# Two graph layers on one core: the loads that bring activations back in natural layout move from SyncE's queue to GpSimd's

## The chip, the cores and the metric

The kernel runs on one core of a Trainium2 chip. The metric is the device time of one execution in microseconds (us). The kernel before took 1773.51 us (median of three runs, 1772.94 to 1775.36).

## The reference

The input `x` is 16 batches of 1024 nodes by 128 features, `adj` a 1024 x 1024 matrix, all float32. Two layers, each with a layernorm, a relu and a residual:

```python
h = jnp.maximum(_layernorm(x), 0.0)
x = x + adj @ (h @ weight) + bias                     # layer 0, per batch
h = jnp.maximum(_layernorm(x), 0.0)                   # layer 1: five steps of a gated unit
for _ in range(5):
    m = adj @ h                                       # m_in and m_out are the same product
    av = concatenate([m, m])
    u3 = h @ u3_w.T + u3_b
    z = sigmoid(av @ w3_w.T + w3_b + u3)
    r = sigmoid(av @ w4_w.T + w4_b + u3)
    hv = tanh(av @ w5_w.T + w5_b + (r * h) @ u5_w.T + u5_b)
    h = (1 - z) * h + z * hv
x = x + h
```

Nearly all arithmetic is the product with `adj`, once a step and batch ("aggregation"), and the products with the small weights ("gates").

## The kernel before, in words

**Tiling.** Four batches make a quad; there are four quads. Two quads are in work at a time (`state[0]` and `state[1]`), and their steps alternate: while one quad aggregates, what the other quad's last step left is stored and fetched. One `step` is an aggregation, then the gates of batch pair A, then those of pair B.

**The aggregation** (`aggregate`, matmuls at L504) is a two-level scheme of seven products by seven: 49 small products, numbered by `place(1)` to `place(49)`. Each has two 128 x 128 x 256 matmuls, which the profile shows as four. `adj`'s sums for 40 of the 49 products do not stay in SBUF: they stream from DRAM through `ring`, 12 slots, which are six pairs. One DMA of 512 KB brings a pair (`stream`, 20 pairs an aggregation, 440 in all). It is issued after the second product of a pair, into that pair's slots, so it is needed six pairs later. The last four of an aggregation and the first of the next are put at places in the gates (`GATE_LOADS`).

**Two layouts.** Gates work on `hT` (features on partitions). The aggregation wants the natural layout (nodes on partitions) in `nat[:, k]`, k = 0 to 3 a batch. So after a step VectorE transposes 32 x 32 squares of `hT` (`squares_to_dram`, L669), one DMA of 512 KB stores them to a DRAM scratch (`fn`), and `natural_from` loads the scratch back in four DMAs of 128 KB, each to 32 partitions in runs of 1 KB. Sixteen such loads fill `nat` for one aggregation. Sources are `fn` (a step's result), `ft` and `h` (the layernorm's output of layer 1 and layer 0, parked in DRAM). The output of a finished batch is fetched by the same function into `ho`.

**Who reads nat.** ScalarE copies (L401) and VectorE sums (L238, L241) make the left operands in `big` from it. The first four pieces for the next aggregation are placed in the gates just ahead of it (`GATE_PLACES`: the first copy, of k = 0, at "Az0", the second, of k = 1, at "Az1", the sums of k = 2 and 3 at "Bz1"). The last reads of `nat[:, 0]` and `nat[:, 1]` are the VectorE sums at places 18 and 19 of the running aggregation (`bigs[5]`), those of `nat[:, 2]` and `nat[:, 3]` the ScalarE copies at places 25 and 26 (`bigs[6]`).

**What sets the order.** The author writes out the program order of every engine: `put(k, piece)` hangs a piece on a place and `place(k)` emits it there. `pin` keeps it in that order on its engine. Nothing ties instructions of different engines except semaphores for data and for buffers. All DMAs are issued by SyncE through `dma` (L129), so a DMA that waits holds up those behind it. In a usual step the four groups of loads into `nat` are put at places 48, "Ar0", "Ar1" and "Ar3" of the step that runs (`loads_at`), which is the end of the aggregation and the first gates. GpSimd does only the `pow` of the layernorms (L344), 34 instructions, the last of them at 990 us, and a few set-up instructions.

Of the kernel before, what the change touches and what calls it, by code (L numbers as in the profile page):

```python
# [96 lines left out]
def tile_two_gnn_layers(  # L97
# [9 lines left out]
    nc = tc.nc  # L107
    pin = tc.keep_in_program_order
# [19 lines left out]
    def dma(out, in_):  # L128
        pin(nc.sync.dma_start(out=out, in_=in_))  # L129
# [522 lines left out]
    def by_blocks(hN, k):  # L652
        return hN[bass.ts(k, SQ)].rearrange("y a j e -> y a (j e)")
# [19 lines left out]
    def natural_from(blocks, hN):  # L673

        for k in range(NSQ):
            dma(by_blocks(hN, k), blocks[k])

    parked = {}
    x1s = {}
# [35 lines left out]
    def output(b, blocks):  # L715
        box = {}

        def load():
            box["h"] = flip_tile(f"ho_{b}")
            natural_from(blocks, box["h"])  # L720
            box["x1"] = x_tile(f"1_{b}")
            dma(box["x1"], x1s[b])

        def rest():
            x1 = box["x1"].rearrange("p j (a e) -> p a j e", e=SQ)
            for g in range(NH):
                js = bass.ts(g, CH)
                add(x1[:, :, js], x1[:, :, js], box["h"][:, :, js])

        def store():  # L730
            dma(by_slots(out[b]), box["x1"])

        return load, rest, store
# [244 lines left out]
    def loads_of_next(source, places):  # L978

        for k, at in enumerate(places):  # L980
            put(at, lambda k=k: natural_from(source[k], nat[:, k]))
# [294 lines left out]
```

## Time and profile before

| what | value |
|---|---|
| median of three runs | 1773.51 us |
| the profiled execution's own time | 1770.63 us |
| its span, first to last instruction | 1768.9 us |
| TensorE busy | 1759.2 us, 99% of the span |
| VectorE, ScalarE busy | 1375.1 us (78%), 898.1 us (51%) |
| GpSimd busy | 58.8 us (3%) |
| DMA engines busy, mean of 16 | 70%, 224 GB/s over the span |
| granted TensorE clock | 0.999 |

The span is what the profile sees of one execution; the profiled execution took 1.7 us more than its span. Busy shares are averages over the whole run. A busy DMA share of 1.00 in a window means that all 16 DMA engines had a packet under way all the time.

### The profile page before, as it was taken

The numbers are of one execution on the slowest core, as the hardware profiler recorded it, in microseconds if no ns is written. First come the engines' busy times: TensorE is split into PE (matmuls) and PEld (weight loads), VectorE is DVE, ScalarE is ACT, GpSimd is POOL, SyncE is SP. The second block draws the span as 40 slices with busy tenths as digits, with TensorE's granted clock in tenths as the row PEclk, the third lists the DMA queues.
The fourth block names the chain that finished last, engine by engine and source line by source line (L and its number), as shares of the span: only waits on it lengthen the run. The fifth ranks groups of instructions, "written<-read, shape, count | busy, mean of one in ns | idle before, by whom it ended". The sixth has DMA issues, their size and how long they took to land.

```text
span 1768.9 us, 21409 instructions
## 1 busy us (share of the span) xinstructions
PE 1759.2 (99%) x6438; PEld 1201.1 (68%) x6438; DVE 1375.1 (78%) x2806; ACT 898.1 (51%) x1974; POOL 58.8 (3%) x41
## 2 busy tenths in 40 slices
PE   9999999999999999999999999999999999999998
PEld 3557667588585776858857667585775858667584
DVE  6778888777878687887687968777687777868787
ACT  5246555544555555554455554545455454544544
POOL 3101000000000000000000000000000000000000
PEclk9999999999999999999999999999999999999999
DMA  7499786677496956749749577494866749476684
GB/s 256 157 309 316 228 259 212 181 245 247 127 298 192 284 193 198 237 137 294 226 149 328 177 225 282 151 294 159 248 211 194 252 133 295 166 230 230 193 294 170
DMA packets 169970, 396.88 MB, mean 224 GB/s; under 512 B 18560, under 2 KB 88064, under 8 KB 169856
## 3 DMA queue, kind: packets, MB, share of 16 engines
q1 hardware_dynamic: 169856, 395.52, 70.1%
q8 instruction: 52, 0.85, 0.2%
q14 instruction: 62, 0.51, 0.1%
HBM read 314.44 MB, written 81.00 MB: 224 GB/s over the span
## 4 chain that ended last, share of the span: by engine, by line
PE 96%; DVE 1%; DMA 1%; POOL 1%; ACT 0%; issue 0%; SPq 0%; DVEq 0%; POOLq 0%
PE a L504 27%; PE c L504 14%; PE b L504 7%; PE a_a L504 3%; PE pr_2B L808 2%; PE pr_1B L808 2%; PE pr_0B L808 2%; PE pr_3B L808 2%; PE pr_3A L808 2%; PE pr_2A L808 2%; PE pr_0A L808 2%; PE pr_1A L808 2%; PE pr_4A L808 2%; PE pr_4B L808 2%; PE a_a L620 2%; PE pv_3A L808 2%
## 5 line engine op out<-in xcount | busy, mean ns | idle before, releaser
L504 PE MATMUL a<-ring,big 128*128 128x256 f32 x1120 | 287.9, 380 | 0.3 <-ACT Z L523 0.3
L523 ACT COPY Z<-a 128x256 f32<-128x256 f32 x480 | 177.0, 371 | 193.2 <-PE a L504 193.0
L241 DVE TENSOR_TENSOR Z<-Z,taps 128x512 f32<-128x512 f32 (+1 forms) x264 | 144.6, 554 | 166.3 <-ACT taps L523 166.1
L504 PE MATMUL c<-ring,little 128*128 128x256 f32 x960 | 246.5, 379 | 0.0
L504 PEld LDWEIGHTS a<-ring,big 128*128 128x128 f32 x1120 | 212.2, 190 | 37.4 <-issue 8.1
L241 DVE TENSOR_TENSOR mT<-mT,Z 128x1024 f32<-128x1024 f32 x154 | 188.3, 1223 | 22.9 <-ACT Z L523 17.3
L504 PEld LDWEIGHTS c<-ring,little 128*128 128x128 f32 x960 | 182.2, 190 | 25.1 <-ACT taps L523 0.2
L523 ACT COPY taps<-c 128x256 f32<-128x256 f32 x280 | 103.6, 370 | 116.3 <-PE c L504 111.5
L504 PE MATMUL a<-resident,little 128*128 128x256 f32 x560 | 143.8, 379 | 0.0
L504 PE MATMUL a<-ring,little 128*128 128x256 f32 x560 | 143.7, 379 | 0.0
L504 PE MATMUL b<-ring,big 128*128 128x256 f32 x560 | 143.7, 379 | 0.0
L504 PEld LDWEIGHTS a<-resident,little 128*128 128x128 f32 x560 | 106.3, 190 | 14.7 <-ACT Z L523 0.3
L504 PEld LDWEIGHTS a<-ring,little 128*128 128x128 f32 x560 | 106.4, 190 | 14.4
L504 PEld LDWEIGHTS b<-ring,big 128*128 128x128 f32 x560 | 106.5, 190 | 14.4
L669 DVE STREAM_TRANSPOSE sq<-hT_all 128x512 f32<-128x512 f32 x152 | 98.6, 687 | 0.0
L241 DVE TENSOR_TENSOR little<-big 128x256 f32<-128x256 f32 x154 | 64.2, 417 | 21.4 <-ACT big L401 21.2
L401 ACT COPY big<-nat 128x512 f32<-128x512 f32 x132 | 80.7, 614 | 0.1
L523 ACT COPY taps<-b 128x256 f32<-128x256 f32 x140 | 52.0, 371 | 55.4 <-PE b L504 54.5
L238 DVE TENSOR_TENSOR little<-little,big 128x256 f32<-128x256 f32 x154 | 65.4, 425 | 6.7
L238 DVE TENSOR_TENSOR little<-big 128x256 f32<-128x256 f32 x154 | 64.3, 418 | 0.0
L238 DVE TENSOR_TENSOR little<-big,little 128x256 f32<-128x256 f32 x154 | 64.3, 418 | 0.0
L523 ACT COPY mT<-a 128x256 f32<-128x256 f32 x80 | 29.8, 372 | 48.3 <-PE a L504 48.3
(282 smaller groups left out, 2911.1 us busy)
## 6 DMA issues: line engine op xcount, KB each, us to landing
ring<-rd SPq DMA_DIRECT2D x440, 512.0 KB, 5.8
fn<-sq SPq DMA_DIRECT2D x76, 512.0 KB, 3.9
nat<-fn SPq DMA_DIRECT2D x256, 128.0 KB, 5.7
x1d<-xt SPq DMA_DIRECT2D x16, 512.0 KB, 5.4
sqt<-ft SPq DMA_DIRECT2D x16, 512.0 KB, 6.9
xt<-x1d SPq DMA_DIRECT2D x16, 512.0 KB, 7.0
xt<-in_x_dram SPq DMA_DIRECT2D x15, 512.0 KB, 5.7
out_dram<-xt SPq DMA_DIRECT2D x14, 512.0 KB, 7.6
```

Of the source, the lines that this page charges most:

```text
L238: pin(nc.vector.tensor_sub(o, a, b))
L241: pin(nc.vector.tensor_add(o, a, b))
L401: return [lambda i=i: pin(nc.scalar.copy(made_of(k, i), part(a, b, i))) for i in range(2)]
L504: nc.tensor.matmul(bank, l, right[:, c, :], start=opens and c == 0, stop=c == SB - 1, skip_group_check=True,)
L523: pin(nc.scalar.copy(to, bank))
L620: nc.tensor.matmul(bank, left[:, c, :], right[c // SB][:, c % SB], start=p in (1, 2, 5) and c == 0, stop=c == CH - 1, skip_group_check=True,)
L669: pin(nc.vector.transpose(squares_of_half(sq, g), transposed_half(hT, g)))
L808: nc.tensor.matmul(bank, w_sb[:, w, :], moving, start=start, stop=stop, skip_group_check=True)
```

## The change

One line of `natural_from` (L673 to L676). The four loads of each group are issued from GpSimd's queue:

```diff
     def natural_from(blocks, hN):
 
         for k in range(NSQ):
-            dma(by_blocks(hN, k), blocks[k])
+            pin(nc.gpsimd.dma_start(out=by_blocks(hN, k), in_=blocks[k]))
```

The instructions of TensorE, VectorE and ScalarE and their order stay as they were. SyncE issues 384 DMAs less (256 `nat<-fn`, 48 `nat<-ft`, 32 `nat<-h`, 48 `ho<-fn`), and GpSimd issues them in the same order among themselves, between its `pow` instructions. Twelve loads of the last step (`ho_last`, in `fetch`) stay on SyncE.

## The prediction

> **What bounds the kernel now.** I read the page from the top: busy shares, the chain that ended last, then the waits of TensorE.
>
> ```profile
> span 1768.9 us, 21409 instructions
> PE 1759.2 (99%) x6438; PEld 1201.1 (68%) x6438; DVE 1375.1 (78%) x2806; ACT 898.1 (51%) x1974; POOL 58.8 (3%) x41
> PE 96%; DVE 1%; DMA 1%; POOL 1%; ACT 0%; issue 0%; SPq 0%; DVEq 0%; POOLq 0%
> ```
>
> TensorE (PE) is the chain; it idles 9.7 us in all. The waits of PE between 115 and 1725 us, which is from the first streamed aggregation to the last, are one line:
>
> ```profile
> PE a L504 <- ACT Z L523: 0.3, 1, 0.3
> ```
>
> So there is nothing to win where the changed loads work: a faster load can take away 0.3 us. The question is what it can cost. PE never waits for `ring` or `nat` today, so I look for how near it is to waiting, in one usual step (aggregation from 1146.6 to 1189.0 us, gates to 1223.2). First, all engines by stretches (columns: length, PE, PEld, DVE, ACT, POOL busy, clock, DMA share, GB/s); a quiet aggregation's window and one of nearly pure natural loads follow:
>
> ```profile
> 1146.60:1162.90 16.30, 16.30 (x77) 14.37 (x76) 14.76 (x28) 7.38 (x19) 0.00 (x0) 1.00 0.80 263
> 1162.90:1172.50 9.60, 9.60 (x47) 8.45 (x46) 6.43 (x14) 5.10 (x13) 0.00 (x0) 1.00 1.02 305
> 1172.50:1178.50 6.00, 6.00 (x29) 5.29 (x28) 3.62 (x9) 2.61 (x7) 0.00 (x0) 1.00 0.96 366
> 1199.00:1223.20 24.20, 24.20 (x57) 10.64 (x56) 20.25 (x34) 12.57 (x20) 0.00 (x0) 1.00 0.18 65
> ...
> 840.00:856.40 16.40, 16.40 (x78) 14.47 (x77) 11.15 (x24) 6.70 (x18) 0.00 (x0) 1.00 0.68 215
> 1184.00:1187.50 3.50, 3.50 (x18) 3.08 (x17) 3.21 (x5) 1.59 (x5) 0.00 (x0) 1.00 0.80 183
> ```
>
> The DMA engines are full in the middle of an aggregation and nearly idle (0.18) in the gates. Then SyncE's timeline there, and the landing times of the DMAs on `ring` (min/median/max):
>
> ```profile
> 1178.21 0.43 SPq L129 DMA_DIRECT2D out_dram<-xt  x1
> 1178.69 10.44 SPq L129 DMA_DIRECT2D nat<-fn  x12
> 1189.24 0.38 SPq L129 DMA_DIRECT2D ring<-rd  x1
> 1189.71 1.80 SPq L129 DMA_DIRECT2D nat<-fn  x4
> ```
>
> ```profile
> DMA to landing us min/median/max: 2.4/5.7/10.3
> ```
>
> The natural loads leave SyncE from 1178.7 to 1191.5, behind the aggregation's other DMAs.
>
> **Part 1: what SyncE loses.** 384 issues at 0.42 us (median of `nat<-fn`), 161 us of SyncE's time. It is worth 0 to PE, by the wait list: `ring` DMAs already land before their use. The last four `ring` DMAs of an aggregation no longer stand behind `nat` groups and go out some us earlier; they are needed in the next aggregation, 30 us later. Nothing.
>
> **Part 2: when the loads start.** On SyncE a load's place in the program is also its time. On GpSimd hardly anything stands ahead of it (34 `pow`, all before 992 us), so it starts when its data and its room are ready:
>
> ```profile
> 1162.92 0.69 DVE L238 TENSOR_TENSOR big<-nat,big 128x512 f32<-128x512 f32 x1
> 1163.86 0.68 DVE L238 TENSOR_TENSOR big<-nat,big 128x512 f32<-128x512 f32 x1
> ```
>
> ```profile
> 1169.49 0.62 ACT L401 COPY big<-nat 128x512 f32<-128x512 f32 x1
> 1170.35 0.62 ACT L401 COPY big<-nat 128x512 f32<-128x512 f32 x1
> ```
>
> These are the last reads of `nat[:, 0]`, `[:, 1]` and of `[:, 2]`, `[:, 3]`. The last source, the `fn` store issued at 1155.2, lands 5.9 us later, at 1161.1. So the sixteen loads can start at 1163.6 instead of 1178.7: **15 us earlier, out of the slack stretch and into the full one**. The `ho` loads (issued at 1160.95, at place 16) move the other way: their room comes free in the gates before, where DMA is idle.
>
> **Part 3: what an issue costs on GpSimd.** The trace shows no DMA from GpSimd. From below, SyncE's 0.42 us for the same DMA; from above, GpSimd's own `pow` on 128 x 8, 1.65 us median (up to 2.45 beside VectorE). Neither row is nearer in kind, so I take their geometric middle, sqrt(0.42 x 1.65) = 0.83, call it 0.9 us. Both ends go into the range. Sixteen take 14.4 us, 1163.6 to 1178.
>
> The Trainium skill, *DMA: Bandwidth & Descriptors*, "Specifications", gives about 1 us to the first byte from GpSimd against 0.6 us from SyncE; if that were the price of each issue, the excess of 4.6 us worked out below would be 4.1 (estimate), and the sum hardly different. No row here shows it.
>
> **Part 4: the DMA engines in that stretch.** A `ring` DMA of 524 KB comes every 42.4/20 = 2.12 us and takes a share of 0.68 in the quiet window: 1.44 us of all engines. A natural load takes 0.80/183 GB/s x 131 KB = 0.57 us: 16 are 9.2 us. In 14.4 us the ring asks 0.68 x 14.4 = 9.8, the loads 9.2: 19.0 in 14.4, **4.6 us too much**. Someone's data comes later by that.
>
> What the ring can bear: its DMA goes out when a pair is done and is needed five pairs later, 5 x 2.12 = 10.6 us. It lands after 5.7 in the median: slack 4.9 us. The longest landing of 10.3 us left 0.3.
>
> The 22 aggregations by what else moves:
> - Six (the first, the last, four quiet ones): 4.6 is under 4.9 or there is no such load. 0.
> - Eight with a layernorm's store. Its first tile, four 128 KB DMAs, comes at place 22, 2.3 us of DMA time; four of the eight also store `x1d`, 1.44. Excess 6.9 or 8.3, beyond the slack 2.0 or 3.4: 4 x 2.0 + 4 x 3.4 = 21.6 us.
> - Eight with an output. `ho` has left, the `xt<-x1d` load stays: 4.6 + 1.44 = 6.0, beyond the slack 1.1: 8.8 us.
>
> Together **30.4 us, if the ring bears all of the delay, and 0 if the natural loads bear it**. No row shows two busy queues side by side. I take half, 15.2 us, as neither queue has a claim over the other here. Delay of the natural loads themselves is free: they land by 1183 or so, and the first reader is the copy for "Az0" at 1197.4.
>
> The skill's same page, "Queues, rings and completion order", says each DMA engine goes round between the queues that have work, packet by packet. That would be equal shares, so nearer to the half than to either end; by it the sum stays 15.2. Against the change speaks *SBUF — State Buffer*, "Who interferes with whom": VectorE in a two-port mode keeps GpSimd from writing descriptors. It also says `tensor_tensor`, most of VectorE's work here, has no such mode, so I expect little of it. If it stretched an issue to 2 us, the loads would be spread over 32 us and most of the 15 us would go.
>
> **Sum.** 1770.6 (this execution) + 15.2 - 0.3 = 1785.5. The median of the runs is 2.9 above the profiled execution, so 1788.
>
> **Rivals.**
> 1. *Hidden* (not slower). GpSimd issues slowly enough: at 1.65 us an issue the sixteen take 26 us, in which the ring asks 18.0 and the loads 9.2: 27.2 in 26, an excess of 1.2 us that every slack covers; or the ring's packets go first. It decides from about 1.3 us an issue: there the excess is 2.5, only the four fullest aggregations pass their slack, by 1.3 us, and half of 4 x 1.3 is 2.6 us, too little to tell from no change. For it: 4.9 us median slack. Against: the eight output aggregations are at share 1.02 already. 1773.5, PE's floor. Chance 0.30.
> 2. *The loads don't move*: an unseen wait holds GpSimd, and they leave near their old time. Then nothing changes: 1773.5. The program order on GpSimd shows none. Chance 0.06.
> 3. *GpSimd is the bound.* The last loads are due before the sums on `nat[:, 2:4]` at 1215.4. From 1170.1, less 5.5 us landing, that leaves 39.8 us for eight: it decides from 5 us an issue. At 6 us, sixteen take 96 us in a step of 76.6: 20 steps x 19 = 390 us more, 2160 us. The longest GpSimd row is 2.45 us. Chance 0.02.
> 4. *Faster.* The shorter queue on SyncE, and `ho` gone from the fullest stretch. PE has only 0.3 us to give back there, so over 0.2% needs something I don't see. Chance 0.03.
>
> The forecast, slower by ring stalls, has 0.59. Measurement can tell some 0.2% (3.5 us). Part of the forecast lies under that, so I count it in rival 1: slower 0.61, same 0.36, faster 0.03. The range runs from rival 1 less the spread of the runs (1772) to the full 30.4 us and the spread above (1806).
>
> **What would show it.** In the profile after: `nat` issues on POOL from about place 19, 15 us earlier; their duration (0.9 expected, wrong if over 1.3); DMA share 1.0 from place 19 to the end of the aggregation and lower in the first gates; `ring` landing median above 5.7 with a maximum beyond 10.6; PE waits at L504 for "DMA ring<-rd" of 1 to 4 us in store and output aggregations, none in quiet ones and none for `nat`. If PE's wait list stays at 0.3 us while the loads did move, part 4 is wrong; if the waits name `nat` or `big`, part 3 is.

## The result and the profile after

The changed kernel takes 1854.73 us (median of four runs, 1849.58 to 1855.29), the kernel before, run beside it, 1773.90 us. The ratio is 1.0451, 95% interval 1.0439 to 1.0463: 4.5% slower. The profiled execution of after took 1855.3 us with a span of 1853.4 us, 84.5 us more than the span of before. The forecast was slower, 1788 us, at most 1806.

Page of after: span, busy shares, chain of waits by engine, the two busiest DMA queues.

```profile
span 1853.4 us, 21560 instructions
PE 1788.0 (96%) x6438; PEld 1204.8 (65%) x6438; DVE 1375.8 (74%) x2806; ACT 899.0 (49%) x1974; POOL 269.9 (15%) x425
PE 81%; DMA 15%; DVE 1%; POOL 1%; ACT 1%; issue 0%; SPq 0%; DVEq 0%; POOLq 0%; ACTq 0%
q1 hardware_dynamic: 114560, 345.16, 55.0%
q0 software_dynamic: 18432, 50.36, 10.6%
```

TensorE's work is the same 6438 matmuls, but its share falls from 99% to 96%, and 15% of the chain is now DMA where it was 1%. The 384 moved loads are a queue of their own (q0). TensorE's waits (us in total, times, longest):

```profile
PE a L504 <- DMA ring<-rd: 32.9, 26, 4.6
PE b L504 <- DMA ring<-rd: 8.2, 10, 2.6
PE c L504 <- DMA ring<-rd: 7.2, 3, 4.3
PE a_a L504 <- DMA ring<-rd: 3.2, 4, 1.2
PE a L504 <- ACT taps L523: 2.0, 4, 0.5
```

Where before had one wait of 0.3 us, 45 waits for `ring`, 52.4 us in all (a fifth line of 0.9 us is not shown), stand now. None is for a load into `nat`. The same quiet aggregation in both kernels shows the mechanism. First GpSimd's timeline after (start, us, what, xcount, in brackets its idle time and what ended it), in an aggregation that begins at 418.9 us:

```profile
436.49 4.36 POOL L676 DMA_DIRECT2D nat<-fn  x8 [39.14 <-DVE little L238]
442.74 1.64 POOL L676 DMA_DIRECT2D nat<-fn  x3 [1.89 <-ACT big L401]
444.76 0.55 POOL L676 DMA_DIRECT2D nat<-fn  x1 [0.38 <-DMA nat<-fn]
446.23 1.10 POOL L676 DMA_DIRECT2D nat<-fn  x2 [0.92 <-ACT Z L523]
448.04 0.55 POOL L676 DMA_DIRECT2D nat<-fn  x1 [0.71 <-DMA nat<-fn]
449.09 0.55 POOL L676 DMA_DIRECT2D nat<-fn  x1 [0.50 <-DMA nat<-fn]
```

Then SyncE before, in the same aggregation, which begins at 407.3 us there:

```profile
438.94 6.89 SPq L129 DMA_DIRECT2D nat<-fn  x12
446.12 0.34 SPq L129 DMA_DIRECT2D ring<-rd  x1
446.70 1.96 SPq L129 DMA_DIRECT2D nat<-fn  x4
```

The first load leaves 17.6 us into the aggregation instead of 31.7, 14 us earlier. What DMA makes of it after, the quiet stretch ahead of the loads first (length, PE, PEld, DVE, ACT, POOL busy, clock, DMA share, GB/s):

```profile
418.90:436.50 17.60, 17.60 (x84) 15.51 (x83) 12.42 (x26) 7.21 (x20) 0.01 (x1) 1.00 0.67 210
...
438.00:457.00 19.00, 18.07 (x83) 15.30 (x82) 11.19 (x22) 8.83 (x23) 7.24 (x14) 1.00 1.01 259
457.00:463.30 6.30, 6.04 (x28) 5.01 (x28) 3.55 (x6) 2.23 (x6) 0.00 (x0) 1.00 1.02 393
```

For 19 us all engines are full and move 259 GB/s, `ring` and natural loads together. Then the loads are done, and the same full engines move 393 GB/s: `ring` catching up. Of 259 x 19.0 = 4.92 MB, 2.10 MB are the sixteen loads, so `ring` got 2.82 MB, 5.4 DMAs, where TensorE used up 19.0/2.12 = 9.0 (at the mean of one in 2.12 us). It fell 3.6 DMAs behind, and TensorE stood still in this quiet aggregation too, three times here:

```profile
453.15 1.10 PE L504 MATMUL a<-ring,big 128*128 128x256 f32 x4 [0.41 <-DMA ring<-rd]
...
456.50 1.13 PE L504 MATMUL b<-ring,big 128*128 128x256 f32 x4 [0.52 <-DMA ring<-rd]
...
458.76 1.10 PE L504 MATMUL a<-ring,big 128*128 128x256 f32 x4 [0.26 <-DMA ring<-rd]
```

Landing times (min/median/max) of the `ring` DMAs, then of the 384 moved loads, after:

```profile
DMA to landing us min/median/max: 2.4/6.7/18.6
```
```profile
DMA to landing us min/median/max: 2.7/8.0/11.5
```

A landing of 18.6 us where a `ring` DMA has 10.6 us until it is needed is a stall.

**Where the 84.5 us are.** 52.4 are the waits for `ring`. 15.4 are a half clock: seven stretches, 30.7 us together, in which the granted clock was 0.5 (experiment 7). 3.5 more are waits for ScalarE. 5.0 are longer records of single matmuls outside these stretches, nearly all directly after a wait (worked out from the trace's matmul records). Of the other 8.2, some 7.5 are overlap, from the same records: back to back, a matmul's record begins 0.16 us before the one ahead of it ends, and after each of 46 waits outside the half clock it doesn't. Under 1 us has no name.

### The profile page after: what moved, and what is told of

Its sections match the earlier page's. It is cut to its first block, busy times and chain, and to the rows that moved or that the text cites. A ratio compares the mean times of both kernels' runs of the same rounds, so it can differ in the third digit from the quotient of the medians.

```text
span 1853.4 us, 21560 instructions
## 1 busy us (share of the span) xinstructions
PE 1788.0 (96%) x6438; PEld 1204.8 (65%) x6438; DVE 1375.8 (74%) x2806; ACT 899.0 (49%) x1974; POOL 269.9 (15%) x425
## 3 DMA queue, kind: packets, MB, share of 16 engines
q0 software_dynamic: 18432, 50.36, 10.6%
## 4 chain that ended last, share of the span: by engine, by line
PE 81%; DMA 15%; DVE 1%; POOL 1%; ACT 1%; issue 0%; SPq 0%; DVEq 0%; POOLq 0%; ACTq 0%
PE a L504 21%; DMA ring<-rd 15%; PE c L504 10%; PE b L504 5%; PE pr_3A L808 2%; PE pr_3B L808 2%; PE pr_2B L808 2%; PE pr_1B L808 2%; PE pr_0B L808 2%; PE pr_1A L808 2%; PE pr_0A L808 2%; PE pr_2A L808 2%; PE a_a L504 2%; PE pr_4B L808 2%; PE pr_4A L808 2%; PE a_a L620 1%
## 5 line engine op out<-in xcount | busy, mean ns | idle before, releaser
L504 PE MATMUL a<-ring,big 128*128 128x256 f32 x1120 | 294.9, 386 | 36.7 <-DMA ring<-rd 32.9
L676 POOL DMA_DIRECT2D nat<-fn x256 | 140.4, 553 | 508.0 <-ACT Z L523 268.1
L504 PEld LDWEIGHTS b<-ring,big 128*128 128x128 f32 x560 | 106.4, 191 | 26.9 <-DMA ring<-rd 12.7
L504 PEld LDWEIGHTS a<-resident,little 128*128 128x128 f32 x560 | 107.5, 192 | 15.2 <-ACT Z L523 0.3
L676 POOL DMA_DIRECT2D ho<-fn x48 | 26.2, 552 | 391.6 <-DMA fn<-sq 242.1
L241 DVE TENSOR_TENSOR little<-big 128x256 f32<-128x256 f32 x154 | 64.4, 418 | 21.4 <-ACT big L401 21.4
L344 POOL TENSOR_TENSOR rstd_b<-ve_b,mhalf 128x8 f32<-128x8 f32 x16 | 28.0, 1752 | 279.2 <-DVE ve_b L343 268.2
```

Source lines behind the costliest of these rows:

```text
L241: pin(nc.vector.tensor_add(o, a, b))
L344: pin(nc.gpsimd.tensor_tensor(self.rstd[:, part], self.ve[:, part], mhalf[:, part], ALU.pow))
L504: nc.tensor.matmul(bank, l, right[:, c, :], start=opens and c == 0, stop=c == SB - 1, skip_group_check=True,)
L676: pin(nc.gpsimd.dma_start(out=by_blocks(hN, k), in_=blocks[k]))
```

## The experiments

"Early" below means from place 19 on, as the change does it; "held" means not before the engines reach the place in the program where the group stood. That is not the old time: SyncE ran ahead of the other engines there. In most aggregations the first held load of kernel 1 starts 42.8 to 43.7 us in, where before started it at 31.7 to 35.7. Loss is against the runs of before beside the same kernel. The columns by kind are the lengthening of the aggregations against before, from the first to the last matmul at the aggregation's line, worked out from the trace: four quiet, eight with a layernorm's store, eight with an output. The first and the last aggregation are in no column; the last lost 4.4 us in after, 5.2 in kernel 4 and 7.3 in 5b.

| kernel | median us | loss | ring waits | quiet 4 | store 8 | output 8 |
|---|---|---|---|---|---|---|
| after | 1854.7 | 80.8 | 52.4 | 10.2 | 38.1 | 31.6 |
| 1 all on GpSimd, held | 1784.0 | 10.4 | 0.4 | 2.6 | 1.3 | 0.8 |
| 2 all on SyncE, early | 1870.8 | 97.2 | 67.1 | 6.7 | 39.0 | 49.3 |
| 3 only `ho` on GpSimd | 1775.5 | 1.8 | 1.4 | 0.0 | 0.0 | 0.0 |
| 4 half of `nat` early | 1803.9 | 30.3 | 22.5 | 0.0 | 7.4 | 16.3 |
| 5a one load per 0.87 us | 1856.7 | 82.9 | 61.7 | 7.1 | 36.9 | 35.8 |
| 5b one load per 1.73 us | 1800.3 | 26.5 | 17.5 | 0.0 | 16.2 | 5.9 |
| 6a one DMA, 128 partitions, 4 KB runs | 1786.5 | 12.7 | 10.1 | 0.0 | 13.3 | 1.3 |
| 6b four DMAs, 32 neighbours, 4 KB runs | 1840.3 | 67.9 | 46.7 | 5.5 | 31.7 | 29.0 |
| 6c one DMA, 128 partitions, 1 KB runs | 1792.4 | 20.0 | 14.3 | 0.0 | 19.4 | 1.8 |
| 6d four DMAs, 32 spread, 4 KB runs | 1777.5 | 4.4 | 3.5 | 0.0 | 4.5 | 0.4 |
| 6e four DMAs, 128 partitions, 1 KB runs | 1781.7 | 8.6 | 7.8 | 0.0 | 10.0 | 1.0 |
| 6f the change, order 0, 2, 1, 3 | 1835.8 | 62.4 | 40.4 | 6.2 | 30.3 | 25.9 |

My theory after the result: the loads start 15 us early and take DMA time from `ring`. The rivals: GpSimd's queue itself, its issue price, and the form of the loads.

### 1 and 2: the queue or the time of start

Kernel 1 leaves all loads on GpSimd, and a one-column copy ahead of each group (of what ScalarE or VectorE has just written, `latest`) keeps it from leaving before these engines are at its place:

```diff
+    def natural_from(blocks, hN, hold=True):
+        if hold and latest:
+            pin(nc.gpsimd.tensor_copy(out=tick, in_=latest[-1]))
```

> All changed loads stay on GpSimd's queue, but ahead of each group GpSimd copies one column that the engines write at the place where the group stands in the program, so it can't start earlier than SyncE started it. Theory TIME (the loads hurt because they now run beside the ring's stream in the middle of an aggregation): PE's waits for ring go from 52 us to under 3, the time is 1771 to 1780 us. Theory QUEUE (a second queue, or its descriptors, takes DMA time from the ring whenever it runs): the waits stay, over 1800 us.

Kernel 2 issues all from SyncE, but at the early places:

```diff
+        early_at = (19, 20, 26, 38 if block or me == (2, 0) else 27)
-            loads_of_next(source, loads_at)
+            loads_of_next(source, loads_at if me == (0, 0) else early_at)
```

> All changed loads go back to SyncE, but stand at places 19, 20, 26 and 27 of the aggregation (38 for the last group where its source is stored at 36), about when GpSimd starts them. Theory TIME: most of the loss comes without GpSimd, 1830 to 1860 us, with PE waits for ring in each aggregation. Theory QUEUE: in one queue the ring's DMAs wait only for the natural loads ahead of them, 1773 to 1793 us.

Measured: 1784.0 us for kernel 1 (ratio 1.0062, 1.0045 to 1.0078), above the 1780 that was expected at most, with 0.4 us of `ring` waits; 1870.8 us for kernel 2 (1.0549, 1.0528 to 1.0570), with more `ring` waits than the change. Waits of TensorE in kernel 1, then in kernel 2, then what holds ScalarE in kernel 1 and its first loads in the quiet aggregation, which begins at 408.5 us there:

```profile
PE pv_2A L815 <- ACT z_2A L836: 3.4, 3, 2.1
PE a_a L505 <- ACT Z L524: 2.0, 2, 1.1
```
```profile
PE b L505 <- DMA ring<-rd: 34.2, 14, 4.5
PE c L505 <- DMA ring<-rd: 19.5, 12, 3.1
PE a L505 <- DMA ring<-rd: 9.8, 7, 3.0
```
```profile
ACT big L402 <- DMA nat<-fn: 14.7, 8, 2.9
451.32 2.18 POOL L683 DMA_DIRECT2D nat<-fn  x4
```

Kernel 2 makes the loss with one queue, from the early start alone; how much of its larger loss is due to `ring` DMAs that stand behind loads in that queue I didn't separate. Kernel 1 shows that the loss goes when the loads come late. As they then run mostly in the gates, 11 us later than before in this aggregation, it doesn't show by itself that a second queue does little harm beside `ring`; kernel 6d below does (3.5 us of `ring` waits). The 10 us that kernel 1 still loses are of another kind: ScalarE's copies of `nat`, which waited for no load before, wait 14.7 us for the late ones, and TensorE's waits for ScalarE grow by 6.8 us, one of them followed by 3.41 us of half clock (experiment 7). What is due to the added copies I didn't separate.

### 3 and 4: which loads

```diff
+            natural_from(blocks, box["h"], nc.gpsimd)
```

> Only the 48 output loads (ho) go to GpSimd; the 336 loads into nat stay on SyncE at their places. Theory TIME: ho starts in the idle gates, no new wait, 1771 to 1776 us. Theory QUEUE: an eighth of the loss, about 1784 us.

Kernel 4 leaves the groups k = 0 and 1 of `nat` (and the `ho` loads) early and holds k = 2 and 3:

```diff
-            put(at, lambda k=k: natural_from(source[k], nat[:, k]))
+            put(at, lambda k=k: natural_from(source[k], nat[:, k], k >= 2))
```

> All on GpSimd; the groups k = 0 and 1 start as early as in the change, the groups k = 2 and 3 are held to their old places by the copy of a column. Theory TIME with a slack of 4.9 us ahead of the first wait: half of the loads make under a third of the loss, 1775 to 1800 us. If the loss is in proportion to the loads that run beside the ring, about 1814 us.

Measured: 1775.5 us for `ho` alone (1.0011, 1.0002 to 1.0021), so the `ho` loads cost nearly nothing. Half of `nat` early: 1803.9 us (1.0170, 1.0155 to 1.0185). Half of the loads cost 30 of 81 us, 37%, between the third that was expected at most and the half of a price per load. The quiet aggregations lose nothing where the change loses 10.2 us: a backlog half as large stays within their slack. That is how a limit with a slack behaves; in the other aggregations the two can't be told apart.

### 5: the issue price and rival 1's point

One load per product (0.865 us, the price that the prediction took), or per two (1.73 us), each held by a one-column copy as in kernel 1:

```diff
+                for n in range(NSQ):
+                    p = 19 + PACE * (NSQ * k + n)
+                    put(p, lambda k=k, n=n: natural_from(source[k], nat[:, k], True, n))
```

> All loads on GpSimd and from place 19 on as in the change, but one natural load per product (a one-column GpSimd copy of what ScalarE or VectorE has just written goes ahead of each), so that one leaves every 0.865 us, which is the 0.9 us that the prediction took for an issue, where the change gave 0.55. Theory A (the prediction's sum was right, only the issue price was wrong): the loss falls to the forecast's 15 us, at most its 30, 1789 to 1804 us, and the four quiet aggregations lose nothing. Theory B (what counts is that 16 loads share the DMA engines with ring, whose share falls to about 150 GB/s whenever natural packets wait; the loads took 19 us to land even when issued in 12): pacing to 14 us changes little, quiet aggregations still lose 2 us each, 1835 us or more.

> As the run with one load per product, but one load per two products, 1.73 us each, sixteen in 28 us: rival 1's own point of 1.65 us an issue. Rival 1's sum (9.2 us of DMA time for 16 loads beside ring at 0.68) says the excess of about 1 us is covered: 1773 to 1778. Theory B, with natural and ring packets in each other's way: a natural load is 0.57 us in each 1.73, 0.33 of the engines beside 0.68, so quiet aggregations lose under 1 us, but the store and output ones, with 2 to 4 us more of DMA time, still stall: 1785 to 1800. If it is above 1820, neither holds, and the place of the first loads (19, 20) is what matters.

Measured: 1856.7 us (1.0468, 1.0450 to 1.0487) and 1800.3 us (1.0156, 1.0141 to 1.0172). Theory A falls: at the very pace that the prediction assumed, the loss is 83 us and not 15, and the quiet aggregations lose 1.8 us each. The issue price was not what failed (the change's own sixteen issues took 13.1 us, 436.5 to 449.6, as the later ones waited in part for earlier loads). At 1.73 us rival 1's sum holds in the quiet aggregations and all but one with an output (0.0 each), and fails where a store comes on top (16.2 us).

### 6: the form of the loads

All these start early on GpSimd. Kernels 6a to 6e leave out the re-ordering of the 32 x 32 squares, so they move the same bytes to other places. Kernel 6a, one 512 KB DMA of whole rows for each group of four:

```diff
-        for k in range(NSQ):
-            pin(nc.gpsimd.dma_start(out=by_blocks(hN, k), in_=blocks[k]))
+        pin(nc.gpsimd.dma_start(out=hN.rearrange("p a j e -> p (a j e)"), in_=blocks["all"]))
```

> The change with each group of four loads (four times 32 partitions in runs of 1 KB) replaced by one DMA of the same 512 KB, 128 partitions in runs of 4 KB, at the same place on GpSimd. This leaves out the re-ordering of the 32 x 32 squares, so the values differ, the amount of data and the instructions of the other engines don't. Theory of the pattern (a natural load takes 0.57 us of all engines for 131 KB where ring's packets take 1.44 us for 524 KB, so 9.2 us would become 5.8): the excess in 14 us falls by 3.4 us and the loss to a third, 1775 to 1800 us. Theory of the bytes (any 2.1 MB beside ring in these 15 us make it late): 1835 to 1860.

It gave 1786.5 us (1.0078, 1.0061 to 1.0096). As many bytes, at the same time, from the same queue: the bytes alone cost a sixth. Whole rows change three things, so three kernels take them one by one. 6b: `out=hN[bass.ts(k, SQ)]`, whole rows to 32 neighbouring partitions. 6c: 128 partitions, 1 KB runs.

> The change with its four loads of 128 KB to 32 partitions each, at the same places on GpSimd, but from whole rows of the scratch: runs of 4 KB instead of 1 KB. This leaves out the re-ordering of the squares, so values differ. It takes apart what whole rows of 128 partitions changed together (1854.7 to 1786.5 us). Theory of the destination (a load to 32 partitions slows the packets of both queues): the loss stays, 1835 to 1860 us, and 250 to 280 GB/s while the loads run. Theory of the runs (pieces of 1 KB in DRAM slow them): as with whole rows, 1780 to 1800 us, and over 340 GB/s.

> The other half: one DMA of 512 KB to all 128 partitions at the same places on GpSimd, but in runs of 1 KB from four places of the scratch (values differ, as the squares come to other partitions). Theory of the destination: 1780 to 1800 us and over 340 GB/s while the loads run. Theory of the runs: 1835 to 1860 us, 250 to 280 GB/s. If both halves lose, it is any departure from the ring's own form.

6d: as 6b, but every fourth partition. 6e: four DMAs to all 128 partitions.

```diff
-                    out=hN[bass.ts(k, SQ)].rearrange("y a j e -> y (a j e)"),
-                    in_=blocks["all"][bass.ts(k, SQ)],
+                    out=hN.rearrange("(y k) a j e -> k y (a j e)", k=NSQ)[k],
+                    in_=blocks["all"].rearrange("(y k) f -> k y f", k=NSQ)[k],
```

> Four loads of 128 KB to 32 partitions in runs of 4 KB, as in the run with 4 KB runs to 32 partitions (1840.3 us), at the same places, but the 32 partitions are every fourth one (k, k+4, ... k+124) instead of 32 neighbours (values differ from the reference). Theory of neighbours (32 neighbouring partitions share a path into SBUF, which both queues' packets then wait for): 1780 to 1800 us, over 340 GB/s while the loads run. Theory of the number (many small DMAs of 32 rows each, wherever they go): 1830 to 1850 us, 260 to 290 GB/s.

> Four loads of 128 KB, each to all 128 partitions, in runs of 1 KB on both sides (column blocks of the scratch; values differ). As many DMAs and issues as the change, but none to 32 partitions. Theory of the destination: between 1780 and 1805 us (packets of 1 KB instead of 4 may cost some of it), over 330 GB/s. Theory of the number of DMAs: 1830 us or more.

Measured: 6b 1840.3 (1.0381, 1.0366 to 1.0397), 6c 1792.4 (1.0104, 1.0087 to 1.0121), 6d 1777.5 (1.0027, 1.0016 to 1.0039; below the 1780 to 1800 expected), 6e 1781.7 us (1.0047, 1.0029 to 1.0065). What costs most is the 32 neighbours: four DMAs to them lose 67.9 us, to every fourth partition 4.4. The number of DMAs isn't it (one loses 12.7 us, four spread ones 4.4), and runs of 1 KB add less, 12.9 us between 6b and the change, 7.3 between 6a and 6c. 6d also reads other rows of the scratch than 6b, every fourth one; but the change and 6b are slow and 6a, 6c, 6d and 6e are not, with whole rows and 1 KB pieces on both sides. Windows of the same aggregation while the loads run, 6b and then 6d:

```profile
431.50:452.00 20.50, 20.50 (x96) 17.79 (x94) 12.52 (x25) 9.87 (x26) 7.72 (x16) 1.00 1.00 279
```
```profile
424.50:441.00 16.50, 16.50 (x78) 14.54 (x77) 9.44 (x19) 8.13 (x22) 8.37 (x16) 1.00 0.96 347
```

Both are full; one moves 279, the other 347 GB/s (after: 259). In 6d the sixteen issues go through without a wait for an earlier load:

```profile
424.57 4.19 POOL L685 DMA_DIRECT2D nat<-fn  x8 [38.80 <-DVE little L239]
430.83 4.18 POOL L685 DMA_DIRECT2D nat<-fn  x8 [2.08 <-ACT big L402]
```

The trace's packet records show the same from below: a 4 KB packet of `ring` has a median of 159 ns in the quiet stretch, of 235 beside the change's loads, and of 159 beside 6d's (means 207, 240 and 172).

The Trainium skill, *SBUF — State Buffer*, "Door 1: The DMA port swizzle (why `[64,N]` ≈ `[32,N]`)", says that a DMA's rate goes with how many of 16 ports its partitions reach: 32 neighbours reach 8, partitions 0-63 the same 8, and by its formula every fourth partition reaches all 16. 6b against 6d agrees. If the ports are what counts, the loads' order alone should matter in the change itself: partitions 0-31, then 64-95, which lie on the other ports.

```diff
-        for k in range(NSQ):
+        for k in (0, 2, 1, 3):
```

> The change with the four loads of each group issued in the order k = 0, 2, 1, 3, so that neighbours in the queue go to partitions 0-31, 64-95, 32-63, 96-127 instead of 0-31, 32-63, 64-95, 96-127; everything else, the output too, is as in the change (1854.7 us). Theory of shared ports (partitions 0-63 share one half of the ways into SBUF, 64-127 the other, and packets that wait there hold up both queues): two loads in flight now use both halves, and the loss falls by a third or more, 1780 to 1825 us, with over 290 GB/s while the loads run. Theory that any load to 32 neighbouring partitions is slow by itself, whatever runs beside it: 1845 to 1860 us, 260 GB/s.

Measured: 1835.8 us (1.0345, 1.0328 to 1.0362), 271 GB/s from 435 to 454 us, the stretch that matches the 259 of the change. The loss falls from 80.8 to 62.4 us, by 23%: neither theory's number. Meeting in the same half may explain that part; most of the loss stays with loads to 32 neighbours whatever their order. What of that lies in a port and what in the order in which the engines take packets stays open.

### 7: the half clock

The kernel before, with GpSimd copying a resident operand onto itself ahead of one product, 1 to 8 times, in 19 aggregations:

```diff
+            if (i, p) == (4, 7):
+                pin(nc.gpsimd.tensor_copy(out=tick, in_=latest[0]))
+                for _ in range(COPIES[n]):
+                    pin(nc.gpsimd.tensor_copy(out=right, in_=right))
```

> The kernel before, with one TensorE wait of chosen length in 19 aggregations: ahead of product 7 of the fifth seven, GpSimd copies that product's resident right operand onto itself, 1 to 8 times, and TensorE waits for it. Nothing else moves, and DMA has more time than before. Theory of the clock: waits of 1.8 us and less cost only themselves and some 0.2 us of restart, waits of 2.1 us and more are followed by 3.41 us (or 6.83) at a granted clock of 0.5 and cost 1.7 us (or 3.4) more. With some 12 waits above 2.1 us the time is before + the sum of the waits + 20 to 30 us. Rival: the half clock in the changed kernel comes from something else (DMA load, its power); then the time is before + the sum of the waits + under 5 us, and the records show the full clock.

Measured: 1863.1 us, 89.2 more than before. TensorE's waits for the copies are two lines:

```profile
PE a L512 <- POOL resident L509: 54.9, 17, 6.0
PE a_a L512 <- POOL resident L509: 5.2, 2, 2.6
```

That is 60.1 us. After one wait of 3.96 us (528 to 537 us of this kernel), first PE's timeline, then the stretches:

```profile
529.83 2.07 PE L512 MATMUL a<-resident,little 128*128 128x256 f32 x4 [3.96 <-POOL resident L509]
531.70 1.56 PE L512 MATMUL c<-ring,little 128*128 128x256 f32 x4
533.10 1.03 PE L512 MATMUL b<-ring,big 128*128 128x256 f32 x4
```
```profile
529.40:532.80 3.40, 2.97 (x7) 2.43 (x8) 0.00 (x0) 0.37 (x1) 0.38 (x1) 0.50 0.70 280
532.80:537.00 4.20, 4.20 (x21) 3.68 (x21) 2.92 (x5) 1.69 (x5) 0.00 (x0) 1.00 0.45 117
```

Four matmuls take 2.07 us instead of 1.03, and the clock column reads 0.50 and then 1.00. There are twelve such stretches, eight of 3.41 us and four of 6.83 us, 54.6 in all, so 27.3 us are lost: 60.1 + 27.3 = 87.4 of 89.2. The rival falls: here the loads are where the kernel before has them, and the half clock comes all the same. My bound of 2.1 us was too sharp: all ten waits of 3.28 us and more were followed by a half clock, two of seven between 2.0 and 2.6 us, neither of two at 1.3. Elsewhere it is less sharp: waits of 3.35 us in 6a, 3.29 in kernel 4 and 3.24 in 6c were followed by none, one of 1.90 in kernel 2 by one.

The same in after, at a wait of 4.37 us (528.7 to 533.1 us there):

```profile
528.00:533.10 5.10, 0.73 (x5) 0.34 (x3) 1.36 (x3) 0.70 (x2) 0.00 (x0) 1.00 1.03 264
533.30:536.70 3.40, 3.40 (x9) 2.69 (x9) 1.30 (x2) 0.38 (x2) 0.00 (x0) 0.50 1.01 287
536.70:540.00 3.30, 3.30 (x16) 2.91 (x16) 2.15 (x4) 1.49 (x4) 0.00 (x0) 1.00 1.03 412
```

DMA is full in all three, 264, 287 and 412 GB/s: TensorE stands, runs at half, and then runs. The Trainium skill, *TensorE: Matmul & The Clock Gate*, "Part 1: The HAM clock gate (the "warmup" mystery)", describes a free-running window of about 3.4 us and a half clock after an idle one. The stretches of 3.41 us agree; here a wait of 2.0 us was already followed by one.

## Why the prediction was wrong, point by point

- **Bound** (nothing to win): right. No run here beat before.
- **Part 1** (SyncE's freed time is worth 0): right, so far as the runs tell: kernels 1 and 3 take 384 and 48 issues off SyncE and gain nothing.
- **Part 2** (15 us earlier, into the full stretch): right, 14 us in the aggregation shown. Kernels 1 and 2 show that the loss needs it, and 6d, which starts as early and loses 4.4 us, that it needs the 32 neighbours too.
- **Part 3** (0.9 us an issue): 0.55 us, and 0.60 at most in the `nat<-fn` loads. It didn't matter (5a). No issue was stretched to 2 us, so the rule on two-port modes that the prediction weighed shows no effect here.
- **Part 4**: this failed, in three terms.
  1. *"I take half, 15.2 us, as neither queue has a claim over the other here."* The packets were shared nearly evenly: `ring` had 2.82 of 4.92 MB. But equal packets don't halve the delay. While the loads run, both queues together move 259 GB/s, little more than the 247 that `ring` alone needs (524 KB in 2.12 us), so that the loads come late as well takes next to nothing off `ring`'s delay. The halving took 15.2 us off, and nothing of that shows in the waits. No run tests this term by itself.
  2. *"4.6 us too much."* The prices from stretches with one stream (1.44 us a `ring` DMA, 0.57 us a natural load) don't add up when mixed. In the 19 us shown, 5.4 `ring` DMAs and 16 loads would be 5.4 x 1.44 + 16 x 0.57 = 16.9 us by them; the engines were busy for 1.01 x 19.0 = 19.2 us. By the packet records it is `ring`'s price that rose: 1.91 us a DMA here, and 0.53 a load; beside 6d's loads a `ring` DMA takes 1.38. (The 1.44 isn't what its row gives, either: 0.68 at 215 GB/s is 1.66 us for 524 KB. It comes near 1.36, from the row where `ring` fills the engines, 1.02 at 393 GB/s.) At the end `ring` lacked 3.6 x 1.44 = 5.2 us, above the slack of 4.9 that was to cover quiet aggregations. They were put at 0 and lengthened by 10.2; the output ones were put at 8.8 in full and lengthened by 31.6; the store ones 21.6 and 38.1. The waits for `ring` are 52.4 us where the full sum said 30.4. In 6d, with the loads as early but spread, they are 3.5.
  3. *No term for what a stall brings after it.* Half the clock for 30.7 us is 15.4 us, and slower first matmuls, waits for ScalarE and the rest, mostly lost overlap, are 5.0, 3.5 and 8.2 us.

  Together: 84.5 measured less the 14.9 forecast is 69.6 = 37.2 (`ring` waits, 52.4 less 15.2) + 15.4 + 5.0 + 3.5 + 8.2 + the 0.3 us of gain that wasn't there.
- **Rival 1** (hidden): its point was sound for most aggregations without a store (5b), but 0.55 us an issue is far below the 1.3 us from which it decides, and it made too little of the stores. (Its own excess is 0.8 us, not 1.2: sixteen at 1.65 us are 26.4 us, for which its 18.0 stands.) Rivals 2, 3 and 4 didn't occur.
- **Range**: its upper end was the full excess of 30.4 us. It held neither a price for mixing nor one for the clock, though the view of before had a row with both streams that I should have priced from: 249 GB/s at a share of 1.04 in the last quarter of this aggregation.

```profile
424.50:439.00 14.50, 14.50 (x69) 12.75 (x68) 7.74 (x17) 7.33 (x19) 0.00 (x0) 1.00 0.76 244
439.00:449.40 10.40, 10.40 (x50) 9.16 (x49) 7.71 (x13) 4.46 (x12) 0.00 (x0) 1.00 1.04 249
```

Before, in the stretch where the change starts the loads (first row), DMA is busy for 0.76 and moves 244 GB/s, which is what `ring` needs. Where natural loads run beside the last `ring` DMAs (second row), the engines are full at hardly more.

## What to carry to other kernels

A DMA's place on a busy queue can be what keeps it out of the way: moved to an idle engine, it starts as soon as data and room allow, so ask first what runs at that time. Price a stretch with two streams by a row that has both, give the whole excess to the stream with a deadline where the mixed rate is hardly above its need, and add the clock for TensorE waits beyond some 2 to 3 us. If loads must overlap a stream, let them reach partitions all over SBUF: the same bytes spread over every fourth partition cost 4.4 us, to 32 neighbours 67.9.

## What the runs showed of the hardware that I had not expected

- Loads to 32 neighbouring partitions slow the other queue's packets too: 4 KB packets of `ring` took 235 ns in the median instead of 159, and both queues together moved 259 GB/s (279 with runs of 4 KB, and 347 with these spread over every fourth partition).
- GpSimd issues a 128 KB load in 0.55 us, a 512 KB one to 128 partitions in 0.53 us (runs of 4 KB) or 0.75 us (runs of 1 KB).
- A TensorE wait of 3.3 us or more nearly always, one of 2.0 to 2.6 us sometimes, is followed by 3.41 or 6.83 us at a granted clock of 0.5, which adds 1.7 or 3.4 us to the wait where TensorE works through it.
